# Scan tiles one column wider: a shifted C product, state copies on ScalarE, and a fourth B product on GpSimd

## The chip, the cores and the metric

The kernel runs on one core of a Trainium2 chip. A core has five engines that work side by side, each through its own queue in order: TensorE (PE) multiplies matrices, VectorE (DVE), ScalarE (ACT) and GpSimd (POOL) do elementwise work, and SyncE (SP) issues most of the DMAs. [...] The metric is the device time of one execution in microseconds; the median of three runs before the change is 10453.09 us (10444.79 to 10455.69).

## What is computed

The reference chains four image layers over a tensor of 4 x 192 x 64 x 64 fp32. Layer 0 runs two Mamba state space models over 4 sequences of 4096 tokens (the second over flipped channels) and adds them. Layer 1 is a normed Mamba, a depthwise convolution and an MLP. Layers 2 and 3 are a gated convolution and a windowed product with an MLP; the change does not touch them. The core of each Mamba is a recurrence over tokens for 384 channels and 16 states:

```python
dt = softplus(dt @ dt_w.T + dt_b)
def step(h, inp):
    dt_t, B_t, C_t, x_t = inp
    dA = exp(dt_t[..., None] * A)
    h = dA * h + (dt_t * x_t)[..., None] * B_t[:, None, :]
    y = einsum('bdn,bn->bd', h, C_t)
    return h, y
```

## The kernel before

Three stages follow each other: `two_mambas` (layer 0), `mamba_block` (layer 1), `conv_and_windows` (layers 2 and 3). The first two share the classes `Mamba` and `Scans`.

**Tiling.** A sequence is cut into pieces of T = 512 tokens. One Mamba over one piece is a unit; layer 0 has 32 pieces and two Mambas, so 32 pairs of units that alternate m0, m1, m0, m1; layer 1 has 32 units. The 384 x 16 states of a unit lie in NQ = 12 "quads" k of 128 partitions (16 channels x 8 states) by 4 columns j. Between pieces of a sequence the last state of each quad is kept in `state[:, k, :]`, 128 x 4.

**One quad.** `load` (L605) brings the rows of dt and of dt * x, spread over partitions, by DMA from DRAM (`dtE`, `dtxE`, two buffers each). `product` (L639) multiplies dtxE, 128 x 4 x 512, by B into a tile: on VectorE, with B in PSUM, into `h` (three buffers), or, for quads k in `shared`, on GpSimd, with a copy of B in SBUF (`Bs`, loaded at L628), into `h_apart` (two buffers in layer 0, one in layer 1). `decay` (L646) makes dA for one column on ScalarE, in one of three PSUM buffers; `step` (L652) scans that column on VectorE, in place, starting from `state`. After the four columns `read` copies the last states to `state` (L664) and multiplies the tile by C in place (L665), both on GpSimd. `sum` (L674) adds over states on TensorE, some steps later, and `skip` (L696, L698) and `gate` (L704) finish every fourth quad.

In layer 0, m0 has `shared` (3, 7, 11) and m1 (2, 5, 8, 11); in layer 1 it is (3, 7, 11).

**The order.** It is written out by hand. `Scans.run` counts steps i, four to a quad. A step issues the decay for i + 2, then the scan of i. At column 2 it issues the GpSimd product of the quad that begins at i + 6, if that one is shared. At column 3 it issues `read`, and the VectorE product of the next quad unless that is shared. Then it issues what was put down for this step with `at` (sums, skips, gates), and then `Behind.tick` adds work of other parts (norm, projection, convolution, output), from lanes, within a budget of TensorE and ScalarE time. A `burst` (a Silu or Softplus of 128 x 1536 between two loads of ScalarE's function table) is only issued at an `edge`: the step i for which i + 2 is the last column of a quad and the next quad is not shared. So `shared` moves bursts too.

Of the work beside the scans, three lines matter here: L861, ScalarE's passes of the layer-0 norm; L865, a 128 x 4 GpSimd instruction between two of these passes; and L517, a GpSimd product of 128 x 1536 (dt * x) that follows the Softplus burst (L516) of a unit to come. L471 is a GpSimd copy of three columns into the front of `raw`, whose other columns ScalarE writes (L483).

Of the kernel before, what the change touches and what calls it, by code (L numbers as in the profile page):

```python
# [14 lines left out]
F32 = mybir.dt.float32  # L15
AF = mybir.ActivationFunctionType
ALU = mybir.AluOpType
# [5 lines left out]
C = 192  # L23
# [10 lines left out]
T = 512  # L34
# [89 lines left out]
def near_convolution():  # L124


    sign = sedenion_signs()
    a, b = ([1 if v == "+" else -1 for v in text] for text in (X_SIGNS, W_SIGNS))
    s, rest = [], []
    for k in range(16):  # L130
        row = [sign[i][k] * a[i] * b[i ^ k] for i in range(16)]
        s.append(1 if sum(row) >= 0 else -1)
        rest.append([i for i in range(16) if row[i] != s[k]])
    return a, b, s, rest
# [285 lines left out]
class Mamba:  # L420
# [211 lines left out]
    def product(self, u, k):  # L632
        apart = k in self.shared
        if apart:
            h = self.work.tile([128, 4, T], F32, name="h_apart", bufs=1 if self.summed else 2)
        else:
            h = self.work.tile([128, 4, T], F32, name="h", bufs=3)
        engine, B = (self.nc.gpsimd, "Bs") if apart else (self.nc.vector, "B")
        engine.tensor_tensor(  # L639
            h, u["rows", k // 2, 1], u[B, k % 2].unsqueeze(1).broadcast_to([128, 4, T]), ALU.mult  # L640
        )
        u["h", k] = h

# [6 lines left out]
    def step(self, u, k, j):  # L650
        h = u["h", k]
        self.nc.vector.tensor_tensor_scan(  # L652
            h[:, j, :],
            u.pop(("dA", k, j)),
            h[:, j, :],
            self.state[:, k, j : j + 1],
            ALU.mult,
            ALU.add,
        )

    def read(self, u, k):

        nc, h = self.nc, u["h", k]
        nc.gpsimd.tensor_copy(self.state[:, k, :], h[:, :, T - 1])  # L664
        nc.gpsimd.tensor_tensor(  # L665
            h, h, u["C", k % 2].unsqueeze(1).broadcast_to([128, 4, T]), ALU.mult
        )

    def sum(self, u, k):
        i, h = k % 4, u.pop(("h", k))  # L670
        if i == 0:
            u["ys"] = self.psum_y.tile([128, T], F32, name="y")
        for j in range(4):
            self.nc.tensor.matmul(  # L674
                u["ys"][32 * j : 32 * j + 32, :],
                self.ex.gather[:, i // 2, :],
                h[:, j, :],
                start=(i == 0),
                stop=(i == 3 and self.summed),
                skip_group_check=not self.summed,  # L680
            )
        if i == 3 and not self.summed:
            c = k // 4
            self.nc.tensor.matmul(
                u["ys"],
                self.skip_w[:, c, :],
                u["xc"][:, c, :],
                start=False,
                stop=True,
                skip_group_check=True,  # L690
            )
# [15 lines left out]
class Scans:  # L707
# [49 lines left out]
    def step(self, i, n):  # L757
        m, u, k, j = self.tile(i)
        _, _, first, before, after = self.units[i // (4 * NQ)]
        if k == j == 0:  # L760
            if first:
                self.nc.vector.memset(m.state, 0.0)
            before()
        to = i + (12 if k % 2 else 8)
        if j == 0 and to < n:
            m2, u2, k2, _ = self.tile(to)
            self.behind.force(lambda: "rows" in u2)
            m2.load(u2, k2 // 2, k % 2)
        if i + self.AHEAD < n:
            m2, u2, k2, j2 = self.tile(i + self.AHEAD)  # L770
            m2.decay(u2, k2, j2)
        m.step(u, k, j)
        if j == 1 and k >= NQ - 2 and i + 8 < n:
            m2, u2, _, _ = self.tile(i + 8)
            m2.spread(u2, k - (NQ - 2))
            self.behind.budget -= 0.85
        if j == 2 and i + 6 < n:
            m2, u2, k2, _ = self.tile(i + 6)
            if k2 in m2.shared:
                self.behind.force(lambda: ("Bs", k2 % 2) in u2)  # L780
                m2.product(u2, k2)
        if j == 3:
            self.behind.force(lambda: ("C", k % 2) in u)
            m.read(u, k)
            if k >= NQ - 2 and i + 8 < n:
                m2, u2, _, _ = self.tile(i + 8)
                o = k - (NQ - 2)
                self.behind.add(0, m2.spread_C(u2, o), Piece())
            if i + 1 < n:
                m2, u2, k2, _ = self.tile(i + 1)  # L790
                if k2 not in m2.shared:
                    m2.product(u2, k2)
            added, skipped, gated = (4, 6, 8) if m.summed else (7, 10, 10)
            if k % 4 == 0 and not m.summed or k + 2 in m.shared and m.summed:
                added += 1 if m.summed else 2
            self.at(i + added, lambda: self.sum(m, u, k))
            if k % 4 == 3:
                c = k // 4
                self.at(i + skipped, lambda: self.skip(m, u, c))
                self.at(i + gated, lambda: m.gate(u, c))  # L800
                if c == ND - 1:
                    self.at(i + gated, lambda: self.gated(u, after))
# [14 lines left out]
def two_mambas(tc, x, gb_ap, m_ins, ex_aps, out, at_first):  # L817

    nc = tc.nc
    nq = T // 128  # L820
    with ExitStack() as ctx:
# [15 lines left out]
        mambas = [  # L837
            Mamba(
                nc, f"m{i}", 4, m_ins[i], const, work, const, work, psum_y, psum_a, dram, ident, ex, behind,
                ((3, 7, 11), (2, 5, 8, 11))[i], xcs=4,  # L840
            )
            for i in range(2)
        ]
# [381 lines left out]
def conv_and_windows(tc, x, sums, packs, aps, walsh, out):  # L1225
# [13 lines left out]
    with ExitStack() as ctx:  # L1239
# [147 lines left out]

        xn, kept, stored, outs = {}, {}, {}, {}
        read, projected, through, closed = set(), set(), set(), set()
        made, back = set(), set()  # L1390
        settled = [0] * NB
# [273 lines left out]
        for b in range(NB):  # L1665
            lanes.until(lambda: settled[b] == NP)
            if b == 0:
                w2 = work.tile([128, NH * T], F32, name="w2", tag="hid", bufs=1)
                weights(w2[: C // 4, : 4 * 3 * 128], NB - 1, NB)
                for j in range(16):  # L1670
                    if w_sign[j] > 0:
                        nc.scalar.activation(sed[:, :, j, :], sed[:, :, j, :], AF.Copy, scale=-1.0)
            if b:
                fetch(b)
            if b + 1 < NB:
                lanes.add(2, prepare(b + 1))
            lanes.add(4, inverse(b))
            for g in range(NP):
                spectrum(b, g)
            for k in range(NP):  # L1680
                n = b * NP + k
                reached[b] = k
                lanes.until(lambda: n < 2 or n - 2 in projected)
                lanes.until(lambda: n < X3 or n - X3 in closed)
                x3 = work.tile([128, 3, NWIN], F32, name="x3", bufs=X3)
                nc.sync.dma_start(x3, kept.pop((b, k)))
                lanes.add(0, project(b, k, product(b, k), x3))
# [4 lines left out]
def program(ctx, tc, aps, packs, out):  # L1692
# [6 lines left out]
    def m_ins(name):  # L1699
        return packs[name], aps[name], aps[f"{name}_in_w"], aps[f"{name}_dt_w"]  # L1700

    walsh = dram.tile([128, 16 + NP, C], F32, name="walsh")
    two_mambas(
        tc,
        aps["x"],
# [141 lines left out]
```

## Time and profile before

| | |
|---|---|
| median of 3 runs | 10453.09 us |
| the profiled execution | 10447.22 us, span 10445.3 us |
| granted TensorE clock, mean | 0.864 |
| scans, 3328 on h and 1280 on h_apart | 1266 and 1262 ns each |
| C products, 832 on h and 320 on h_apart | 4532 and 4530 ns each |
| state copies, 832 and 320 | 192 and 190 ns each |
| B products, VectorE 832, GpSimd 320 | 2261 and 4616 ns each |
| decays dA, 4608 | 686 ns each |

A line of a timeline gives the start and length in microseconds, the engine, the line of the kernel, the operation, the tile written and the tiles read; in brackets how long the engine sat idle before it and whom it waited for. Lengths of neighbours overlap a little, so distances from start to start are what adds up. A line of waits gives who waited for whom, the microseconds in total, the times and the longest. A line of windows gives a stretch, its length, then the busy time (and number of instructions) of PE, its weight loads, DVE, ACT and POOL, the clock, the DMA share and GB/s.

### The profile page before, as it was taken

What the parts mean: (1) busy time and instruction counts of PE and PEld (TensorE: products, weight loads), DVE (VectorE), ACT (ScalarE), POOL (GpSimd) and SP (SyncE); (2) the same over time, 40 slices, a digit from 0 to 9 for tenths busy, and PEclk for the clock granted to TensorE, in tenths of its full rate; (3) what the DMA queues carried; (4) which work ended last, traced back from release to release, by engine and by line L of the source; (5) the groups of instructions that cost most, each with busy time, mean ns of one, the idle gap of its engine ahead of it and who ended that gap; (6) DMA issues with size and microseconds to landing.
All of it is one profiled execution on the core that took longest, in us unless ns stands there. A gap on an engine that the chain in (4) does not pass through costs nothing. (4 is left out here: it accounts for less than half of the span.)

```text
span 10445.3 us, 96318 instructions
## 1 busy us (share of the span) xinstructions
PE 8260.7 (79%) x30264; PEld 3448.8 (33%) x30264; DVE 8758.5 (84%) x7569; ACT 6522.9 (62%) x9370; POOL 7937.2 (76%) x3712
## 2 busy tenths in 40 slices
PE   6777777777777777777558888888888886989898
PEld 2222222222222222222123333333333333545455
DVE  8999999999999999999968888888888876555552
ACT  5766666666666666666556767677776653444433
POOL 6999999999999999999969888888888861101100
PEclk8888888888888888888668999999999987999999
DMA  7777777777777777777656556556555543122110
GB/s 187 198 189 197 192 194 194 197 197 192 190 197 194 193 195 194 199 190 193 165 141 159 158 153 162 153 153 161 153 158 152 154 110 74 44 61 53 41 41 19
DMA packets 1020423, 1605.58 MB, mean 154 GB/s; under 512 B 250965, under 2 KB 284073, under 8 KB 1019401
## 3 DMA queue, kind: packets, MB, share of 16 engines
q1 hardware_dynamic: 1018912, 1596.13, 58.5%
q8 instruction: 240, 3.93, 0.2%
q10 hardware_dynamic: 1000, 3.30, 0.1%
q14 instruction: 271, 2.21, 0.1%
HBM read 1379.66 MB, written 219.41 MB: 153 GB/s over the span
## 5 line engine op out<-in xcount | busy, mean ns | idle before, releaser
L652 DVE TENSOR_TENSOR_SCAN h<-dA,m_state,h 128x512 f32<-128x512 f32 x3328 | 4041.3, 1266 | 231.9 <-ACT dA L646 157.7
L646 ACT ACTIVATE dA<-dtE,m_A 128x512 f32<-128x512 f32 x4608 | 3110.3, 686 | 1633.7 <-DVE h L652 1301.1
L665 POOL TENSOR_TENSOR h<-h,C 128x2048 f32<-128x2048 f32 x832 | 3770.4, 4532 | 72.2 <-DMA C<-r_bc 5.2
L639 DVE TENSOR_TENSOR h<-dtxE,B 128x2048 f32<-128x2048 f32 x832 | 1881.3, 2261 | 67.6 <-DMA dtxE<-r_dtx 66.6
L652 DVE TENSOR_TENSOR_SCAN h_apart<-dA,m_state,h_apart 128x512 f32<-128x512 f32 x1280 | 1554.0, 1262 | 135.4 <-ACT dA L646 123.2
L639 POOL TENSOR_TENSOR h_apart<-dtxE,Bs 128x2048 f32<-128x2048 f32 x320 | 1477.2, 4616 | 0.2 <-PE y L674 0.2
L665 POOL TENSOR_TENSOR h_apart<-h_apart,C 128x2048 f32<-128x2048 f32 x320 | 1449.6, 4530 | 25.8
L674 PE MATMUL y<-h,gather 128*32 128x512 f32 x6656 | 1006.3, 680 | 545.5 <-POOL h L665 399.1
L1382 POOL TENSOR_TENSOR d<-d,rs 128x512 f32<-128x512 f32 x64 | 86.3, 1349 | 1596.7 <-DVE rs L1381 1575.7
L476 PE MATMUL ps_in<-xT,m_in_w 96*128 96x512 f32 x1536 | 925.6, 757 | 322.5 <-ACT z L483 307.3
L560 PE MATMUL ps_conv<-raw,m_conv 128*128 128x512 f32 x1536 | 697.1, 599 | 6.7 <-POOL raw L471 4.2
L476 PEld LDWEIGHTS ps_in<-xT,m_in_w 96*128 96x128 f32 x1536 | 360.3, 244 | 895.3 <-issue 413.2
L476 PE MATMUL ps_in<-xn,m_in_w 96*128 96x512 f32 x768 | 426.7, 695 | 163.1 <-ACT z L483 75.3
L1131 PE MATMUL ps_dw<-strip,dw 96*96 96x512 f32 x1152 | 526.3, 602 | 9.3 <-ACT xc L588 8.5
L674 PEld LDWEIGHTS y<-h,gather 128*32 128x32 f32 x6656 | 140.3, 113 | 1179.4 <-issue 536.7
L377 PE MATMUL ps_h<-xn,t 96*128 96x512 f32 x768 | 422.7, 695 | 131.8 <-ACT xc L588 67.8
L1547 PE MATMUL sed_ps<-xn,sed 64*128 64x256 f32 (+3 forms) x2944 | 488.0, 404 | 7.0 <-DVE y L1566 7.0
L494 PE MATMUL ps_x<-xc,m_pack 128*68 128x512 f32 x576 | 373.8, 802 | 130.5 <-ACT xc L490 130.5
L517 POOL TENSOR_TENSOR raw<-dt,xc 128x1536 f32<-128x1536 f32 x96 | 324.7, 3383 | 185.9 <-ACT dt L516 183.6
L646 ACT ACT_TABLE_LOAD x345 | 442.6, 1283 | 14.8 <-DMA dtE<-r_dt 8.5
L507 PE MATMUL ps_dt<-dbl,m_dt_w 68*128 68x512 f32 x576 | 319.0, 658 | 155.8 <-ACT dt L510 109.2
L664 POOL COPY m_state<-h 128x4 f32<-128x4 f32 x832 | 159.5, 192 | 369.8 <-DVE h L652 362.4
(196 smaller groups left out, 11899.8 us busy)
## 6 DMA issues: line engine op xcount, KB each, us to landing
dtE<-r_dt SPq DMA_DIRECT2D x2304, 256.0 KB, 5.2
dtxE<-r_dtx SPq DMA_DIRECT2D x2304, 256.0 KB, 4.3
r_dt<-dt SPq DMA_DIRECT2D x96, 768.0 KB, 3.9
r_dtx<-raw SPq DMA_DIRECT2D x96, 768.0 KB, 6.2
C<-r_bc SPq DMA_DIRECT2D x192, 256.0 KB, 6.2
Bs<-r_bc SPq DMA_DIRECT2D x128, 256.0 KB, 7.1
x<-x SPq DMA_DIRECT2D x64, 384.0 KB, 3.6
img<-x SPq DMA_DIRECT2D x28, 512.0 KB, 8.4
```

The source lines that it names most:

```text
L377: nc.tensor.matmul(ps, self.w1[:, k, bass.ts(m, 128)], x[:, k, :], start=(k == 0), stop=(k == 1))
L476: nc.tensor.matmul(ps, self.in_w[:, k, bass.ts(e, 128)], xn[:, k, :], start=(k == 0), stop=(k == 1))
L494: nc.tensor.matmul(ps, self.x_w[:, d, :], xc[:, d, :], start=(d == 0), stop=(d == ND - 1))
L517: nc.gpsimd.tensor_tensor(dtx, dt, xc, ALU.mult)
L560: nc.tensor.matmul(ps, self.conv[:, d, j, :], raw[:, d, j : j + T], start=(j == 0), stop=(j == K - 1))
L639: engine.tensor_tensor(h, u["rows", k // 2, 1], u[B, k % 2].unsqueeze(1).broadcast_to([128, 4, T]), ALU.mult)
L646: self.nc.scalar.activation(dA, u["rows", k // 2, 0][:, j, :], AF.Exp, scale=self.A[:, k, j : j + 1])
L652: self.nc.vector.tensor_tensor_scan(h[:, j, :], u.pop(("dA", k, j)), h[:, j, :], self.state[:, k, j : j + 1], ALU.mult, ALU.add,)
L665: nc.gpsimd.tensor_tensor(h, h, u["C", k % 2].unsqueeze(1).broadcast_to([128, 4, T]), ALU.mult)
L674: self.nc.tensor.matmul(u["ys"][32 * j : 32 * j + 32, :], self.ex.gather[:, i // 2, :], h[:, j, :], start=(i == 0), stop=(i == 3 and self. ...
L1131: nc.tensor.matmul(ps, dw[:, k, j, :], s[:, k, dy : dy + rows, dx : dx + HW], start=(j == 0), stop=(j == 8),)
L1547: nc.tensor.matmul(out, sed[p, int(h is not None), i ^ position(k, s), cols], xn[b, g][p, c, :], start=group(t) not in begun, stop=left[gr ...
```

## The change

Both tiles, `h` and `h_apart`, get one column more: 513 in place of 512. The B product writes columns 1 to 512, and the scan works there. The C product reads columns 1 to 512 and writes columns 0 to 511, so column 512, the last state, survives it. The copy to `state` is no longer the first of two GpSimd instructions in `read`; it is an own method, `keep`, on ScalarE, put down for two steps later. The sum reads columns 0 to 511. In layer 0, m0 gets the `shared` of m1. Layer 1 keeps its own.

```diff
-            h = self.work.tile([128, 4, T], F32, name="h_apart", bufs=1 if self.summed else 2)
+            h = self.work.tile([128, 4, T + 1], F32, name="h_apart", bufs=1 if self.summed else 2)
         else:
-            h = self.work.tile([128, 4, T], F32, name="h", bufs=3)
+            h = self.work.tile([128, 4, T + 1], F32, name="h", bufs=3)
         engine, B = (self.nc.gpsimd, "Bs") if apart else (self.nc.vector, "B")
         engine.tensor_tensor(
-            h, u["rows", k // 2, 1], u[B, k % 2].unsqueeze(1).broadcast_to([128, 4, T]), ALU.mult
+            h[:, :, 1:], u["rows", k // 2, 1], u[B, k % 2].unsqueeze(1).broadcast_to([128, 4, T]), ALU.mult
         )
...
         self.nc.vector.tensor_tensor_scan(
-            h[:, j, :],
+            h[:, j, 1:],
             u.pop(("dA", k, j)),
-            h[:, j, :],
+            h[:, j, 1:],
...
+    def keep(self, u, k):
+        self.nc.scalar.copy(self.state[:, k, :], u["h", k][:, :, T])
+
     def read(self, u, k):
 
         nc, h = self.nc, u["h", k]
-        nc.gpsimd.tensor_copy(self.state[:, k, :], h[:, :, T - 1])
         nc.gpsimd.tensor_tensor(
-            h, h, u["C", k % 2].unsqueeze(1).broadcast_to([128, 4, T]), ALU.mult
+            h[:, :, :T], h[:, :, 1:], u["C", k % 2].unsqueeze(1).broadcast_to([128, 4, T]), ALU.mult
         )
...
-                h[:, j, :],
+                h[:, j, :T],
...
             m.read(u, k)
+            self.at(i + 2, lambda: m.keep(u, k))
...
-                ((3, 7, 11), (2, 5, 8, 11))[i], xcs=4,
+                (2, 5, 8, 11), xcs=4,
```

## The prediction

> **What bounds the kernel now.** I read the page first (busy shares and slices), then the windows of two stages, then the waits inside the first stage, and last the timeline of one pair of units, because only there can one see which wait ends last.
>
> ```profile
> PE 8260.7 (79%) x30264; PEld 3448.8 (33%) x30264; DVE 8758.5 (84%) x7569; ACT 6522.9 (62%) x9370; POOL 7937.2 (76%) x3712
> DVE  8999999999999999999968888888888876555552
> POOL 6999999999999999999969888888888861101100
> ...
> 2000.00:3000.00 1000.00, 746.78 (x2541) 284.22 (x2543) 967.26 (x743) 680.87 (x1044) 955.29 (x406) 0.82 0.74 195
> 6000.00:7000.00 1000.00, 876.77 (x2810) 324.80 (x2809) 852.71 (x690) 703.74 (x932) 870.23 (x438) 0.93 0.59 157
> ```
>
> The changed code runs in two stages. In the two-mamba stage (about 75 to 5207 us) VectorE is busy 97% and GpSimd 96%; in the mamba-block stage (to about 8540 us) TensorE, VectorE and GpSimd all stand near 87% and none is full. After that GpSimd is nearly idle and nothing changed runs. So the first stage is a VectorE stage with GpSimd right behind it, and there the waits count:
>
> ```profile
> DVE h_apart L652 <- ACT dA L646: 73.7, 32, 2.5
> DVE h_apart L652 <- POOL h_apart L639: 10.2, 29, 0.5
> ...
> POOL raw L517 <- ACT dt L516: 72.7, 42, 2.3
> POOL m_state L664 <- DVE h L652: 71.8, 82, 2.0
> ...
> ACT xs L861 <- POOL shift L865: 116.7, 29, 4.1
> ```
>
> These are from 200 to 5000 us. VectorE's main loss is about thirty waits of some 2.4 us, one a pair. The timeline shows their source (unit m0 begins with the B product at 2161.78):
>
> ```profile
> 2161.78 2.26 DVE L639 TENSOR_TENSOR h<-dtxE,B 128x2048 f32<-128x2048 f32 x1
> 2168.87 2.26 DVE L639 TENSOR_TENSOR h<-dtxE,B 128x2048 f32<-128x2048 f32 x1
> ...
> 2184.18 3.63 DVE L652 TENSOR_TENSOR_SCAN h_apart<-dA,m_state,h_apart 128x512 f32<-128x512 f32 x3 [0.35 <-POOL h_apart L639]
> 2184.36 4.52 POOL L665 TENSOR_TENSOR h<-h,C 128x2048 f32<-128x2048 f32 x1
> ...
> 2188.85 0.22 POOL L865 TENSOR_SCALAR shift<-shift 128x4 f32<-128x4 f32 x1
> 2189.02 0.18 POOL L664 COPY m_state<-h 128x4 f32<-128x4 f32 x1
> 2189.11 0.45 ACT L861 ACTIVATE xs<-xt,shift 128x192 f32<-128x192 f32 x1 [4.03 <-POOL shift L865]
> 2189.29 4.57 POOL L665 TENSOR_TENSOR h<-h,C 128x2048 f32<-128x2048 f32 x1
> ...
> 2190.26 1.28 DVE L652 TENSOR_TENSOR_SCAN h_apart<-dA,m_state,h_apart 128x512 f32<-128x512 f32 x1 [2.45 <-ACT dA L646]
> ```
>
> A tiny norm instruction (L865) stands behind a 4.5 us C product in GpSimd's queue; ScalarE stops for it 4.03 us, the next decay dA is late, VectorE stands still 2.45 us.
>
> **A budget of one pair.** From start to start in this timeline, four scans take 4.72 us (2164.15 to 2168.87), a VectorE B product 2.37 (2161.78 to 2164.15), a gating product 0.59. Unit m1 (8 of its 12 B products on VectorE) then needs 12 x 4.72 + 8 x 2.37 + 3 x 0.59 = 77.37 us. It took 77.32 (2084.46 to 2161.78): pure VectorE. Unit m0 (9 on VectorE) needs 79.74 and took 83.06 (to 2244.84): 3.3 us are stalls, of which the timeline shows 0.20 + 0.35 + 2.45. A pair is 160.4 us. GpSimd occupies 155.5 of it (160.4 less its waits, (72.7 + 71.8) / 29.9 pairs = 4.8).
>
> [...]
>
> **The change part by part.**
> 1. State copies leave GpSimd. Each is 0.19 us busy and, from its start to that of the C product behind it, 0.27 us (2189.02 to 2189.29). 24 a pair free 6.5 us of GpSimd; 12 a unit free 3.2 us in the mamba block.
> 2. The copies go to ScalarE. No row shows a 128x4 SBUF copy there. Nearest: a 128x4 ACTIVATE with a pointer bias (ln_rs, 243 ns), an accumulator read (187 ns, but 0.09 us from start to start). [...] Bounds 0.1 to 0.25; I take 0.1, so 2.4 us a pair on an engine 68% busy. The copy comes in step i + 2, behind the decay for i + 4, which must itself wait for scan i + 1; the scan it needs is therefore over, and it waits for nothing. Behind it stand decays and, in the same step, the bursts (table load, 1.48 us, table load). After a burst VectorE has 0.2 to 0.4 us of cover (0.97 us from dA's start at 2199.95 to its scan at 2200.92, of which 0.69 is dA), so 0.1 is mostly hidden. Uncovered it would be 0.1 x 6 bursts = 0.6 us a pair.
> 3. Must the copy wait for the C product, which writes the same tile before it? It reads column 512, the product writes 0 to 511. Such a case is in the trace: ScalarE writes columns 3 and up of raw while GpSimd's halo copy of columns 0 to 2, earlier in the program, is still to come:
>
> ```profile
> 1165.86 0.58 ACT L483 COPY raw<-ps_in 128x512 f32<-128x512 f32 x1
> ...
> 1169.17 0.20 POOL L471 COPY raw<-m_halo 128x9 f32<-128x9 f32 x1
> ```
>
> So columns are told apart, and no wait arises. If it did, ScalarE would stop for up to 4.5 us in each of 24 quads.
> 4. m0 gives a fourth B product to GpSimd: VectorE -2.37 us a pair, GpSimd +4.6 (its products at 2044.40, with the next start at 2049.00). GpSimd then needs 155.5 - 6.5 + 4.6 = 153.6 us a pair, VectorE 2 x 77.37 = 154.7. It fits, barely.
> 5. What moves with it. m0 gets m1's order: B2, C0, C1, then L517, L865, C2, B5. From the m1 tail at 2168.8: B2 to 2173.4, C0 2177.9, C1 2182.4, L517 2185.8, L865 2186.0 against 2189.1 now. ScalarE reached its wait at 2185.1, so it loses 0.9 instead of 4.03 us, and VectorE, which wants that dA at 2187.8 at the earliest, next to nothing. GpSimd no longer waits for dt (burst one edge later, as in m1). B5 and B8 end 0.2 to 0.4 us before their scans by the same count, B2 and B11 1 to 3 us. So of 3.3 us of stall I keep 1.1 (the 0.20, the burst delay, near misses of B5 and B8).
> 6. One more Bs load a unit of m0: 32 x 256 KB on SP, 0.60 us of issue each, about 0.26 MB more beside the 31 MB a pair (160.4 us at 195 GB/s). m1 already does this; it lands in 7.1 us, long before B2. Nothing.
> 7. The wider tiles. TensorE reads raw at odd columns (ps_conv, 592 ns median) as fast as aligned h (y, 617). VectorE writes strip in rows starting at odd columns in 689 ns against 668 for an aligned product: 0. GpSimd's C product is the unknown: now it reads and writes rows 513 apart. Of four rows with 1536 elements, the one with aligned inputs and odd output rows takes 3438 ns (L517, two-mamba stage), the others 3082 (L597, input rows 513 apart), 3252 and 3267. So odd rows look neutral to 10% faster; the other reading, that odd output rows cost the 171 ns between the two L517, would be +0.23 for 2048 elements, and more with odd reads as well. I take 0; bounds -0.45 and +0.35 us each.
> 8. The mamba block: GpSimd frees 3.2 us of about 100 a unit, but waits for VectorE already (m_state, 225 us), so the copy is no bound there; TensorE's 45 us of waits for C products may shrink by 32 x 0.27 = 9 us, and 32 x 12 copies on ScalarE (VectorE waits for dA 165 us there) give about as much back. 0, within 20.
>
> Sum: 32 pairs x (2.37 + 2.2) = 146 us. The profiled execution took 10447.2 us (span 10445.3); 10447 - 146 = 10301. The median of the three runs, 10453.1, lies 6 us above it, hence 10307.
>
> **The rivals.**
> Stall stays: L865 is no earlier, because the norm's place or GpSimd's lag moves, and only VectorE's product is saved: 32 x 2.37 = 76 us, 10377. For it: GpSimd's slack falls to 1 us a pair; against: m1 runs in this order without a stall.
> GpSimd gets fuller than it is (slower): the C product at odd columns costs more. From +0.05 us each GpSimd (153.6 + 24 d) takes over from VectorE, at +0.28 the gain is gone, at +0.35 a pair is 162.0: 32 x 1.6 = 51, and some 15 in the mamba block: 10519. For it: the two L517; against: L597 and L595.
> C product faster: GpSimd clears all stalls, 32 x 5.7 = 182, and TensorE waits less in the block, 10: 10261.
> The copies make ScalarE late after most bursts, and GpSimd's fuller m0 adds near misses of B: about 10440.
>
> **How the numbers follow.** Forecast 0.48 (own range 10270 to 10350), stall stays 0.25 (0.04 of it within no change), GpSimd fuller 0.15, C faster 0.08, ScalarE late 0.04. A change of under 0.2% (21 us) can't be told from none. Faster 0.48 + 0.21 + 0.08 = 0.77, same 0.08, slower 0.15. The range from 10250 to 10455 leaves out the slower case and a few hundredths at either end.
>
> **What would show it.** In the changed profile: m0 and m1 both near 77 to 78.5 us; ACT xs <- POOL shift far under 117 us; VectorE's 2.45 us waits gone; L664 gone from GpSimd and a ScalarE copy of 0.16 to 0.25 us in its place with no wait for POOL; C product within 0.1 us of 4.53; GpSimd over 97% busy. I am wrong if the C product's mean moves by more than 0.1 us, if the copy waits, or if VectorE waits for h_apart B products beyond 1 us a pair.

## The result and the profile after

The changed kernel takes 10357.01 us (median of 4 runs, 10353.09 to 10358.94) beside 10453.28 us for the kernel before: ratio 0.9909, interval 0.9892 to 0.9926. The forecast was 10307. So 96 us came where 146 were expected. The profiled span shrank by 88.6 us, from 10445.3 to 10356.7 (the execution profiled before was 6 us under its median, the one after 1.5 us above), and the first normed image of the mamba block (the first L310) and its last strip part this by stage: the two-mamba stage is 109.4 us shorter, the mamba block 23.8 us longer, the last stage 3.0 us shorter.

First the page's busy times of the changed kernel, then its windows in the two stages:

```profile
PE 8231.6 (79%) x30264; PEld 3420.2 (33%) x30264; DVE 8680.6 (84%) x7537; ACT 6649.9 (64%) x10522; POOL 7450.7 (72%) x2592
```

```profile
2000.00:3000.00 1000.00, 759.22 (x2615) 286.33 (x2615) 976.90 (x756) 713.82 (x1211) 922.98 (x272) 0.85 0.75 199
6000.00:7000.00 1000.00, 863.81 (x2763) 318.15 (x2762) 836.12 (x675) 704.61 (x1035) 792.77 (x312) 0.94 0.56 154
```

GpSimd lost 486 us of work, ScalarE gained 127. In the two-mamba stage VectorE is busy 98% and GpSimd 92%; the prediction had GpSimd above 97%. In the block VectorE and TensorE are both busy for a smaller share than before: they wait more there. The reason for the 92% stands in the groups of instructions (line, operation, tiles and count; then busy time in all and the mean in ns; then idle time before them and its cause):

```profile
L667 POOL TENSOR_TENSOR h<-h,C 128x2048 f32<-128x2048 f32 x800 | 3336.1, 4173 | 721.5 <-DVE h L652 546.6 <-issue 82.7 <-DMA dtxE<-r_dtx 43.7
L639 POOL TENSOR_TENSOR h_apart<-dtxE,Bs 128x2048 f32<-128x2048 f32 x352 | 1596.0, 4534 | 27.0 <-DMA Bs<-r_bc 24.0 <-ACT dA L646 2.8
...
L662 ACT COPY m_state<-h 128x4 f32<-128x4 f32 x800 | 145.6, 182 | 0.0
...
L662 ACT COPY m_state<-h_apart 128x4 f32<-128x4 f32 x352 | 63.5, 180 | 2.8 <-DVE h_apart L652 2.8
```

The C product went from 4532 to 4173 ns, which nothing had asked for, and GpSimd now waits for VectorE. The copy on ScalarE lasts 0.18 us and never waits for GpSimd; it waits for VectorE 2.8 us in all. The waits from 200 to 5000 us:

```profile
POOL h L667 <- DVE h L652: 219.8, 146, 2.3
DVE h L652 <- ACT dA L646: 39.5, 34, 1.3
DVE h_apart L652 <- ACT dA L646: 17.1, 24, 0.8
DVE h_apart L652 <- POOL h_apart L639: 2.3, 3, 1.0
ACT xs L864 <- POOL shift L868: 15.4, 29, 0.5
```

ScalarE's wait for the norm's little GpSimd instruction fell from 116.7 to 15.4 us, and VectorE's thirty waits of 2.45 us are gone. Some 60 us of shorter ones are left. In the timeline of one unit m0, from its first product at 2124.93 to that of m1 at 2204.38, they look like this:

```profile
2124.93 2.27 DVE L639 TENSOR_TENSOR h<-dtxE,B 128x2048 f32<-128x2048 f32 x1
...
2160.89 0.32 ACT L921 COPY o<-ps_out 128x192 f32<-128x192 f32 x1 [2.65 <-PE ps_out L913]
2161.83 2.46 DVE L652 TENSOR_TENSOR_SCAN h_apart<-dA,m_state,h_apart 128x512 f32<-128x512 f32 x2 [0.80 <-ACT dA L646]
2162.34 0.18 ACT L662 COPY m_state<-h 128x4 f32<-128x4 f32 x1
2162.53 1.28 ACT L534 ACT_TABLE_LOAD   x1
...
2165.22 0.53 ACT L864 ACTIVATE xs<-xt,shift,rs 128x192 f32<-128x192 f32 x1
2167.79 2.46 DVE L652 TENSOR_TENSOR_SCAN h<-dA,m_state,h 128x512 f32<-128x512 f32 x2 [1.32 <-ACT dA L646]
...
2204.38 2.27 DVE L639 TENSOR_TENSOR h<-dtxE,B 128x2048 f32<-128x2048 f32 x1
```

This m0 took 79.45 us (83.06 before), and the m1 ahead of it, from 2047.61 to 2124.93, 77.32 us as before. The two stalls, 0.80 and 1.32 us, are all that tells m0 from m1 now. Both are ScalarE being late: before the first it had waited 2.65 us for TensorE's ps_out; the second comes after a burst, with a norm pass right behind it.

### The profile page after: what moved, and what is told of

It is laid out like the page before. It is cut to its first block, busy times and chain, and to the rows that moved or that the text cites. A ratio compares the mean times of both kernels' runs of the same rounds, so it can differ in the third digit from the quotient of the medians.

```text
span 10356.7 us, 96620 instructions
## 1 busy us (share of the span) xinstructions
PE 8231.6 (79%) x30264; PEld 3420.2 (33%) x30264; DVE 8680.6 (84%) x7537; ACT 6649.9 (64%) x10522; POOL 7450.7 (72%) x2592
## 5 line engine op out<-in xcount | busy, mean ns | idle before, releaser
L652 DVE TENSOR_TENSOR_SCAN h<-dA,m_state,h 128x512 f32<-128x512 f32 x3200 | 3884.6, 1267 | 256.9 <-ACT dA L646 186.3
L667 POOL TENSOR_TENSOR h<-h,C 128x2048 f32<-128x2048 f32 x800 | 3336.1, 4173 | 721.5 <-DVE h L652 546.6
L639 DVE TENSOR_TENSOR h<-dtxE,B 128x2048 f32<-128x2048 f32 x800 | 1809.8, 2262 | 66.0 <-DMA dtxE<-r_dtx 66.0
L652 DVE TENSOR_TENSOR_SCAN h_apart<-dA,m_state,h_apart 128x512 f32<-128x512 f32 x1408 | 1709.5, 1263 | 85.5 <-ACT dA L646 80.2
L639 POOL TENSOR_TENSOR h_apart<-dtxE,Bs 128x2048 f32<-128x2048 f32 x352 | 1596.0, 4534 | 27.0 <-DMA Bs<-r_bc 24.0
L667 POOL TENSOR_TENSOR h_apart<-h_apart,C 128x2048 f32<-128x2048 f32 x352 | 1468.9, 4173 | 108.0 <-DVE h_apart L652 106.8
L476 PE MATMUL ps_in<-xT,m_in_w 96*128 96x512 f32 x1536 | 846.5, 691 | 97.1 <-ACT z L483 57.2
L476 PE MATMUL ps_in<-xn,m_in_w 96*128 96x512 f32 x768 | 440.9, 715 | 171.9 <-ACT z L483 77.2
L476 PEld LDWEIGHTS ps_in<-xT,m_in_w 96*128 96x128 f32 x1536 | 320.9, 224 | 697.7 <-issue 365.2
L904 PE MATMUL ps_out<-m_pack,xc 128*128 128x192 f32 x1536 | 334.9, 370 | 264.3 <-DVE xc L698 187.1
L377 PE MATMUL ps_h<-xn,t 96*128 96x512 f32 x768 | 419.4, 691 | 137.5 <-ACT xc L588 70.1
L676 PE MATMUL y<-h_apart,gather 128*32 128x512 f32 x2816 | 429.9, 686 | 60.2 <-DVE xc L698 44.9
L517 POOL TENSOR_TENSOR raw<-dt,xc 128x1536 f32<-128x1536 f32 x96 | 325.3, 3389 | 190.7 <-ACT dt L516 189.9
```

The source lines that it names most:

```text
L377: nc.tensor.matmul(ps, self.w1[:, k, bass.ts(m, 128)], x[:, k, :], start=(k == 0), stop=(k == 1))
L476: nc.tensor.matmul(ps, self.in_w[:, k, bass.ts(e, 128)], xn[:, k, :], start=(k == 0), stop=(k == 1))
L639: engine.tensor_tensor(h[:, :, 1:], u["rows", k // 2, 1], u[B, k % 2].unsqueeze(1).broadcast_to([128, 4, T]), ALU.mult)
L652: self.nc.vector.tensor_tensor_scan(h[:, j, 1:], u.pop(("dA", k, j)), h[:, j, 1:], self.state[:, k, j : j + 1], ALU.mult, ALU.add,)
L667: nc.gpsimd.tensor_tensor(h[:, :, :T], h[:, :, 1:], u["C", k % 2].unsqueeze(1).broadcast_to([128, 4, T]), ALU.mult)
L676: self.nc.tensor.matmul(u["ys"][32 * j : 32 * j + 32, :], self.ex.gather[:, i // 2, :], h[:, j, :T], start=(i == 0), stop=(i == 3 and self ...
```

## The experiments

Two questions: which part made the gain, and where the missing 50 us are. One view is that the parts add up, each with a gain of its own. The rival: they only work together. The table puts all runs side by side. "Need" is the prediction's own count of VectorE's work a pair (77.37 us for a unit with 8 B products on VectorE, 79.74 with 9, 75.0 with 7), "waits" are VectorE's waits from 200 to 5000 us divided by the pairs in that stretch, and "pair" is the measured mean distance of the silu bursts of 26 pairs. "Stage" is the start of the first L310, "block" the distance from there to the last strip, each from one profiled execution. The ratio is to the kernel before as it was measured beside each run.

| run | need | waits | pair | stage | block | time | ratio to before, interval |
|---|---|---|---|---|---|---|---|
| before | 157.1 | 3.23 | 160.35 | 5244.1 | 3310.7 | 10453.28 | 1 |
| after | 154.7 | 1.97 | 156.57 | 5134.7 | 3334.5 | 10357.01 | 0.9909, 0.9892 to 0.9926 |
| e1 no fourth product | 157.1 | 3.24 | 160.40 | 5245.4 | 3332.3 | 10469.43 | 1.0021, 1.0013 to 1.0029 |
| e2 only fourth product | 154.7 | 5.87 | 160.44 | 5254.3 | 3304.1 | 10453.27 | 1.0002, 0.9994 to 1.0011 |
| e3 copies on GpSimd | 154.7 | 1.53 | 156.06 | 5118.1 | 3327.4 | 10339.24 | 0.9895, 0.9880 to 0.9909 |
| e7 slow C product | 154.7 | 2.11 | 156.48 | 5136.2 | 3345.6 | 10368.94 | 0.9921, 0.9906 to 0.9936 |
| e10 fast products | 154.7 | 1.62 | 156.09 | 5122.8 | 3334.8 | 10341.85 | 0.9894, 0.9878 to 0.9911 |
| e13 five of twelve | 150.0 | 6.67 | 157.00 | 5142.6 | 3313.0 | 10350.12 | 0.9909, 0.9894 to 0.9924 |
| e14 block undone | 154.7 | 2.00 | 156.47 | 5130.1 | 3324.8 | 10340.98 | 0.9900, 0.9885 to 0.9915 |
| e17 tiles in block | | | | 5125.5 | 3325.0 | 10340.48 | 0.9900, 0.9884 to 0.9917 |
| e12 best of each | 154.7 | 1.54 | 156.08 | 5120.8 | 3304.2 | 10315.29 | 0.9874, 0.9858 to 0.9891 |
| e8 copy in block | | | | 5241.7 | 3317.9 | 10445.10 | 0.9993, 0.9985 to 1.0002 |
| e8x two copies | | | | 5242.9 | 3401.6 | 10529.12 | 1.0074, 1.0059 to 1.0089 |

Need and waits add up to the measured pair within 0.4 us in all ten kernels for which the table has them. So a change in this stage is read by two questions: what does VectorE have to do, and how long does it stand still?

**e1: the changed kernel without the fourth product in m0.**

```diff
-                (2, 5, 8, 11), xcs=4,
+                ((3, 7, 11), (2, 5, 8, 11))[i], xcs=4,
```

> The change without its fourth B product: m0 keeps 3, 7, 11 on GpSimd; shift and ScalarE copies stay. Theory A (order and room together make the gain): in m0 the small norm instruction still stands behind L517, B3 and C1, and L517 waits for dt, so it comes only about 0.9 us earlier (one C product and one copy shorter); VectorE's 2.45 us wait falls to about 1.5; the pair goes from 160.4 to about 159.3, the two-mamba stage gains 35 us, the mamba block loses the 24 us that the change lost there: about 10440. Theory B (the faster C product alone clears the stall): the pair falls to 157.4, 96 us less 24: about 10380.

The time, 10469.43, lies above what either theory gave: nothing is gained, though GpSimd is relieved to 87% from 1000 to 3000 us. Its waits:

```profile
DVE h_apart L652 <- ACT dA L646: 54.5, 31, 1.8
DVE h L652 <- ACT dA L646: 31.4, 60, 1.0
...
ACT xs L864 <- POOL shift L868: 95.4, 29, 3.3
```

GpSimd's free time did not bring the norm's instruction L868 forward. The timeline shows why:

```profile
2175.10 3.43 POOL L517 TENSOR_TENSOR raw<-dt,xc 128x1536 f32<-128x1536 f32 x1 [2.97 <-ACT dt L516]
2178.49 4.51 POOL L639 TENSOR_TENSOR h_apart<-dtxE,Bs 128x2048 f32<-128x2048 f32 x1
2182.95 4.16 POOL L667 TENSOR_TENSOR h<-h,C 128x2048 f32<-128x2048 f32 x1
2187.09 0.23 POOL L868 TENSOR_SCALAR shift<-shift 128x4 f32<-128x4 f32 x1
```

GpSimd stands idle 2.97 us until the Softplus burst has made dt, and then L868 still has a dt * x product, a B product and a C product ahead of it. In the changed kernel it comes straight behind L517. ScalarE's wait went only from 116.7 to 95.4 us, and VectorE got a second kind of wait, 31.4 us where the kernel before has 8.7. The sum of its waits stayed: 96.8 us in both. The freed time alone does not end the stall.

**e2: the kernel before with the fourth product alone**, the same line edited the other way.

> The kernel before with only m0's set changed to 2, 5, 8, 11: no shift, copies on GpSimd. Theory A: GpSimd needs 155.5 + 4.6 = 160.1 us a pair, more than VectorE's 154.7, so GpSimd becomes the bound, VectorE waits for h_apart products, the pair is 160 to 161: 10440 to 10475. Theory B (the new order alone cures the late norm instruction, GpSimd has enough room): pair about 157, about 10345 to 10370, as the mamba block is untouched.

```profile
ACT xc L565 <- PE ps_conv L560: 302.1, 175, 3.6
...
DVE h L652 <- ACT dA L646: 128.6, 103, 1.9
...
DVE h_apart L652 <- ACT dA L646: 42.3, 49, 1.6
```

VectorE has its 2.37 us a pair less to do, and waits 2.64 us more. Theory A's figure holds, though VectorE waits for decays and not, as it said, for h_apart products (2.4 us in all). GpSimd is busy 98% from 1000 to 3000 us: ScalarE waits long for TensorE's convolution, and VectorE for its decay. The new order alone does not cure the norm's late instruction either: it stands straight behind L517 here too, but GpSimd comes to both late, and ScalarE still waits for it 86.3 us. That GpSimd's late C products hold TensorE's queue is the likely link; I did not test it by itself. Neither part alone is worth anything here, and both together are worth 96 us. The rival holds.

**e3: the changed kernel with the copies back on GpSimd**, but behind the C product, which the wider tile allows.

```diff
     def read(self, u, k):
...
+        nc.gpsimd.tensor_copy(self.state[:, k, :], h[:, :, T])
...
-            self.at(i + 2, lambda: m.keep(u, k))
```

> The change with the state copies on GpSimd, behind the C product, none on ScalarE. Theory C (the copies on ScalarE cost the 24 us in the mamba block): the block goes back from 3334 to about 3311 us, the two-mamba stage stays at 157.1 us a pair or gains 0.2 from ScalarE: about 10330. Theory D (the block is slower because C products end earlier and shift what ScalarE and TensorE meet): the block stays near 3334, all about 10357. If the copies also made VectorE's 0.80 and 1.33 us waits in the two-mamba stage, these go and the pair falls to 155.2: 10270.

VectorE's waits fall from 1.97 to 1.53 us a pair, which makes 14 us, and the stage ends 16.6 us earlier in this profile. Over all the profiles of this stage's two forms it ended at 5118 to 5123 us with the copies on GpSimd (e3, e10, e12) and at 5125 to 5136 with them on ScalarE (after, e7, e14, e17). The pair is 156.06 to 156.09 us with the former and 156.47 to 156.57 with the latter. So that place costs about 11 to 16 us, and GpSimd has room for them. The room is about what the quicker product gives, 24 x 0.36 = 8.6 us a pair against 6.5 for the copies; no run tried the copies there with a slow product. The block took 3327.4 us, between theory C's value and theory D's.

**e5: a probe of the GpSimd product**, four times each ahead of everything, with one read start changed at a time. Nothing it computes is used.

```diff
+            nc.gpsimd.tensor_tensor(even, even, by(c0), ALU.mult)
+            nc.gpsimd.tensor_tensor(odd[:, :, :T], odd[:, :, 1:], by(c0), ALU.mult)
...
+            nc.gpsimd.tensor_tensor(far[:, :, :T], far[:, :, 8:], by(c0), ALU.mult)
...
+            nc.gpsimd.tensor_tensor(even, even, by(c1), ALU.mult)
```

> The changed kernel with a bare row of GpSimd products of 128 x 2048 ahead of everything, four of each layout, outputs unused. Theory E (rows of 512 read at a start that differs from the second operand's by an odd column save time): 513 apart, read 1 to 512 and write 0 to 511: 4.17 us; 513 apart in place: 4.2 to 4.4; 520 apart (aligned, shifted by 8): 4.53; plain tile with C at an odd start: 4.2. Theory F (it is the pattern of four separate rows in place of one run of 2048): every padded tile, aligned ones too, takes 4.17, the plain tile 4.53 whatever C's start. Theory G (it is the distance of the write from the read): only the shifted ones, 1, 2 and 8 columns, are faster, those in place are not. The 128 x 4 copies on ScalarE: 0.18 us in both layouts.

The view of single lines (count, then shortest, median and longest in ns); rows are 512 columns apart in p_even, 513 in p_odd, 520 in p_far, and L1733 is the plain tile with C read from column 1:

```profile
L1724 POOL TENSOR_TENSOR p_even<-p_even,p_c x4: 4492/4493/4493, 16.5 to 212.5; 128x2048 f32<-128x2048 f32 x4
...
L1725 POOL TENSOR_TENSOR p_odd<-p_odd,p_c x4: 4147/4150/4150, 21.0 to 216.9; 128x2048 f32<-128x2048 f32 x4
...
L1730 POOL TENSOR_TENSOR p_far<-p_far,p_c x4: 4492/4492/4492, 41.9 to 237.8; 128x2048 f32<-128x2048 f32 x4
...
L1733 POOL TENSOR_TENSOR p_even<-p_even,p_c x4: 3810/3810/3810, 55.3 to 251.3; 128x2048 f32<-128x2048 f32 x4
```

Theories F and G fail: a shift by 8 columns does nothing (L1730: 4492), nor does where the result goes (an odd output start took 4493). E had the right kind of cause, but not the distances that save. What counts is how the two reads start relative to each other: C moved by one column makes the product 0.683 us shorter over four rows, 0.171 a row. Rows 513 apart save 0.343, two rows' worth. All the forms tried fit one rule, that a row is short, by 0.171 us, where the first read starts 2 or 3 columns after the second, counted modulo 4; why, no run shows. The same rule fits the four durations of 1536 elements in part 7 of the prediction: 3438 ns with no short row of three, 3267 and 3252 with one, 3082 with two. L517 is quicker in the block (3267 ns against 3438) because dt lies there in rows 513 apart, not slower elsewhere because of where it writes.

**e7: the changed kernel with the C product slow again**, by tiles 8 columns wider and not 1.

```diff
-            h = self.work.tile([128, 4, T + 1], F32, name="h", bufs=3)
+            h = self.work.tile([128, 4, T + 8], F32, name="h", bufs=3)
...
-            h[:, :, :T], h[:, :, 1:], u["C", k % 2].unsqueeze(1).broadcast_to([128, 4, T]), ALU.mult
+            h[:, :, :T], h[:, :, 8:], u["C", k % 2].unsqueeze(1).broadcast_to([128, 4, T]), ALU.mult
```

> The changed kernel with its tiles 8 columns wider instead of one, written 8 to the left, so that the C product should take the 4.49 us that the probe measured for this form; all else is as in the changed kernel. Theory 'the C product's speed was part of it': GpSimd's work of a pair of units goes from 144.5 to 144.5 + 24 x 0.32 = 152 us, close to VectorE's 154.7, and waits come back: 10385 to 10440. Rival 'its speed is slack': GpSimd stood idle for 8 per cent and only ScalarE is waited for, so 10357 within 10.

Its C products take 4540 ns, as before the change. Its window:

```profile
1000.00:3000.00 2000.00, 1523.96 (x5192) 567.21 (x5190) 1955.63 (x1512) 1429.95 (x2429) 1957.29 (x542) 0.84 0.76 200
```

GpSimd is busy 98% (1957 of 2000 us; 1846 in the changed kernel), VectorE 98% in both, and the stage ends 1.5 us later. In this stage the quicker product was slack. The run is 12 us longer, 2 more than the rival allowed, and 11 of them lie in the block; its ratio's interval overlaps with that of the changed kernel.

**e10: the other way, every GpSimd product quick.** The copies as in e3, tiles 8 columns wider and used from column 1, C and Bs read from column 2.

```diff
-            v = self.work.tile([128, T], F32, name=f"{n}{o}", bufs=bufs)
+            v = self.work.tile([128, T + 2], F32, name=f"{n}{o}", bufs=bufs)[:, 2:]
```

> The copies on GpSimd behind the C product as in the run e3, and all of GpSimd's products (C and B) laid out so that both reads differ by 2 or 3 columns modulo 4 in every row: C 4.17 to 3.81, B 4.53 to 3.81 us. GpSimd's work of a pair falls by 24 x 0.36 + 8 x 0.72 = 14 us. Theory 'VectorE and ScalarE bound the pair now': no gain beyond 10 us on 10339. Rival 'GpSimd's speed still sets it': the pair goes from 156.3 towards VectorE's 154.7, 10339 - 32 x 1.6 = 10290.

C products took 3818 ns and GpSimd's B products 3821, as the rule says, and GpSimd's busy share fell to 85% (1707 of 2000 us). The pair stayed at 156.09 (e3: 156.06). GpSimd's speed does not bound this stage any more.

**e13: five of twelve B products on GpSimd in both mambas**, with these quick products, a third buffer for `h_apart` in that stage, and the block as before.

```diff
-                (2, 5, 8, 11), xcs=4,
+                (2, 4, 6, 8, 10), xcs=4,
```

> Meant to be faster than both: the two-mamba stage with GpSimd's products in the fast layout of e10, copies on GpSimd, and 5 of 12 B products on GpSimd in both mambas; the block as before. Theory 'VectorE bounds the pair': its need falls by 2 x 2.26 us from 154.7 to 150.2, GpSimd's rises to 24 x 3.82 + 10 x 3.82 + 8 + 24 x 0.19 = 142 us, so the pair goes from 156.3 to 151.5 to 153: two-mamba stage 105 to 155 shorter, time 10180 to 10230 with the block at 3311. Rival 'ScalarE's or TensorE's chain bounds it now': the pair stays above 155 and the time above 10290.

```profile
ACT xc L566 <- PE ps_conv L561: 450.9, 183, 4.3
...
DVE xc L703 <- PE y L691: 76.9, 53, 1.7
...
DVE h_apart L653 <- ACT dA L647: 60.2, 42, 2.2
...
DVE h_apart L653 <- POOL h_apart L640: 44.1, 51, 2.1
DVE h L653 <- ACT dA L647: 21.7, 54, 1.4
```

VectorE has 4.7 us a pair less to do, and waits 5 us more: for y, for decays, for GpSimd's products. The rival's figure holds. With VectorE's need at 154.7 us the best pair, 156.06, is within 1.4 us of it; less need has so far come back as waits.

**e8 and e8x: the mamba block's 24 us.** The kernel before, with one or two ScalarE copies of 128 x 4 added for every quad of the block (the texts below say step) at the place of the new one; nothing reads them.

```diff
+    def idle_copy(self, k):
+        if self.summed:
+            self.nc.scalar.copy(self.spare, self.A[:, k, :])
...
+            self.at(i + 2, lambda: m.idle_copy(k))
```

> The kernel before with one ScalarE copy of 128 x 4 added for every step of the mamba block (A to a spare tile, nothing reads it), at the place where the changed kernel has its copy; its own copies stay on GpSimd. Theory 'the copy on ScalarE is what the block gave back': the block goes from 3311 to 3330 to 3336 us and the time to 10473 (10465 to 10480). Rival 'the block's loss comes from the tiles or from GpSimd's order': within 5 of the kernel before, 10453.

> As the run before it, with two such copies for each step in place of one. Theory 'the block's unit locks to a whole number of the 3.41 us stretches in which TensorE's clock is held': the first copy already put every unit on 102.4 us, so the second costs little: the block within 6 us of that with one copy. Rival 'each copy costs what it delays': twice the rise, about 10495 if one copy gives 10473.

With one copy the time is not above that of the kernel before, so the copy alone did not cost the block its 24 us here; its 7 us on the block lie within the spread told below. With two, both theories failed: the block is 91 us longer, neither the same nor twice as much. TensorE's two waits in the MLP of a unit, 1.75 and 2.83 us in the kernel before, are now 2.09 and 3.14:

```profile
7233.68 2.70 PE L377 MATMUL ps_h<-xn,t 96*128 96x512 f32 x4 [2.09 <-ACT hid L382]
7289.78 6.90 PE L377 MATMUL ps_h<-xn,t 96*128 96x512 f32 x8 [3.14 <-ACT xc L589]
```

Here such waits cost more than their own length, as the durations behind them show. The same eight products of ps_h, in two units of the kernel before (first fence) and one of the changed one (second):

```profile
7241.43 3.70 PE L377 MATMUL ps_h<-xn,t 96*128 96x512 f32 x8 [2.83 <-ACT xc L588]
...
7341.82 5.40 PE L377 MATMUL ps_h<-xn,t 96*128 96x512 f32 x8 [2.83 <-ACT xc L588]
```

```profile
7249.25 5.40 PE L377 MATMUL ps_h<-xn,t 96*128 96x512 f32 x8 [2.92 <-ACT xc L588]
```

After the same idle time TensorE needs 3.70 or 5.40 us. The trace records the granted clock, and windows over the two units of the kernel before, with one inside the second, show it (the figure after the five engines):

```profile
7241.43:7245.13 3.70, 3.70 (x9) 1.76 (x10) 1.95 (x2) 1.88 (x3) 3.22 (x3) 1.00 0.74 178
7341.82:7347.22 5.40, 5.40 (x9) 2.35 (x10) 1.94 (x2) 1.88 (x3) 4.85 (x5) 0.68 0.42 109
7342.40:7345.81 3.41, 3.41 (x6) 1.35 (x5) 1.36 (x2) 1.30 (x3) 3.30 (x2) 0.50 0.46 122
```

In the longer case the clock is halved for 3.41 us, from 0.58 us after the restart. The traces record two values of the granted clock, 1.00 and 0.50, and in the kernel before all its changes lie on one grid of 3.413 us through the whole run; so do those of the changed one. The time of the eight products goes with the place on this grid where the restart falls: of the 24 units of the kernel before, all with an idle time of 2.82 or 2.83 us, 6 restart 1.10 to 1.53 us behind a point of the grid and take 3.70 us, the other 18 restart elsewhere on it and take 5.40 us (13 units) or 6.77 to 7.09 (5). What makes the clock fall, no run tested. The restarts of neighbouring units of this kernel are 99.3 to 105.8 us apart, and many fall well and badly by turns. In the changed one the restart comes 0.09 us later and was slow (5.40 us) in all 24 units, and of the 20 distances 13 are 102.4 or 102.5 us. That is 30.0 steps of the grid, so such a unit meets it in the same place again and again: in seven neighbours from 6217.8 us on the half clock begins 0.94, 0.54, 0.41, 0.34, 0.31, 0.30 and 0.58 us after the restart. What holds a unit there, no run tested; e8, with the same idle time of 2.92 us, keeps that distance in 8 of 20 cases only and has three quick restarts, so the premise of the theory before e8x, all units on 102.4 us, did not hold.

The products of the norm and the projection around ps_h meet the half clock too: in the kernel before, four of the norm's (L308) took 1.88 us from 5463.51 on, at a clock of 1.00, and 2.96 us from 5671.12 on, at 0.64. Together with ps_h they were busy 1002.5 us before and 1018.7 after (L476 ps_in 426.7 and 440.9, L377 ps_h 422.7 and 419.4, L308 mean 153.1 and 158.4). But this sum does not explain the block by itself: e8 has the lowest, 985.3, and a block of 3317.9 us. The windows of the whole block, before, after, e12 and e14, show more:

```profile
5244.10:8554.80 3310.70, 2814.08 (x8965) 1047.63 (x8966) 2767.55 (x2227) 2265.74 (x3002) 2817.34 (x1405) 0.90 0.58 153
5134.70:8469.20 3334.50, 2805.93 (x8965) 1035.63 (x8966) 2767.38 (x2227) 2307.73 (x3386) 2616.47 (x1021) 0.91 0.56 152
5120.80:8425.00 3304.20, 2806.94 (x8965) 1042.70 (x8966) 2767.54 (x2228) 2266.14 (x3002) 2817.66 (x1405) 0.91 0.59 153
5130.10:8454.90 3324.80, 2833.46 (x8965) 1057.03 (x8966) 2767.24 (x2228) 2266.17 (x3002) 2818.74 (x1405) 0.90 0.58 152
```

e12 and e14 (below) have the same code in the block, that of the kernel before. e14's is 21 us longer and TensorE's busy time in it 27 us, its idle time 6 us less: there the pace makes the difference. In the changed kernel TensorE is busy 8 us less than before and idle 32 us more. So its 24 us show as waits, and how many of these a slow restart set off is open.

**e14 and e17: the changed kernel with the block's code undone**, wholly (plain tiles, product in place, copy on GpSimd ahead of it), or only the copy brought back to GpSimd.

```diff
+        if self.summed:
+            nc.gpsimd.tensor_copy(self.state[:, k, :], h[:, :, T])
...
-            self.at(i + 2, lambda: m.keep(u, k))
+            if not m.summed:
+                self.at(i + 2, lambda: m.keep(u, k))
```

> The changed kernel with the mamba block alone as it was: there plain tiles, the C product in place, the copy on GpSimd ahead of it. Theory 'the 24 us that the block gave back are due to the change's own code in the block': block 3304 to 3318 us and 10357 - 24 = 10333 (10325 to 10342). Rival 'the block is only hit at another moment of TensorE's clock because the stage ahead of it ends earlier': block stays near 3334 and the time within 5 of 10357.

> The changed kernel with, in the mamba block, the copy back on GpSimd ahead of the C product, and the wider tiles kept: no ScalarE copy there. With e8 (ScalarE copies alone: block 3318) it parts the block's 24 us. Theory 'the ScalarE copy and the rest add up': block 3334 - 7 = 3327, time 10350. Rival 'the copy on ScalarE matters only together with the tiles': block near 3311, time 10333.

Both blocks took 3325 us, between the two theories' values for e14. With the old block code, five profiles (before, e2, e12, e13, e14) gave 3304 to 3325 us; with the new one, three (after, e1, and e5, whose probe runs ahead of everything) gave 3332 to 3334.5. So the code seems to matter, but the same code varies by 21 us from one kernel to another, with different work ahead of it. Against this spread the 24 us cannot be shared out between the copy and the tiles.

**e12: each stage in its shortest form**, the two-mamba stage as in e3 and the block's code as before.

> Each stage in the form that was shortest so far: in the two-mamba stage the wider tiles and the copies on GpSimd behind the C product (as in e3, stage ended at 5118), in the mamba block the code of the kernel before (as in e14). If the stages' times add up: 5118 + a block of 3304 to 3325 + 1887 = 10309 to 10330 of span, time 10312 to 10335, ratio 0.987 to 0.989. If the block's time is mostly a matter of the moment at which it meets TensorE's clock: anywhere from 10312 to 10345, no shorter than e3's 10339 for certain.

10315.29 us, ratio 0.9874 (0.9858 to 0.9891): the fastest kernel of all here, 135 us under the kernel before in the same comparison (10450.34). Against the changed kernel the two ratios differ by 0.35 points, and their intervals just part. The stages' times added up, as the first forecast had it, though the time lies within the rival's range too. e3, e10, e14 and e17 lie near 10340, but their intervals overlap with that of the changed kernel, so none of them is shown to be faster than it.

## Why the prediction was right and where it failed

The side, faster, was right, and the path was right: VectorE bounds the two-mamba stage, the norm's instruction held ScalarE, and m1's order in m0, with the room on GpSimd that it needs, ended that. By the prediction's parts:

- **Parts 1 and 4, GpSimd's room.** Right in effect. With the C product at its old speed, as the sum assumed, GpSimd is 98% busy and the stage is 1.5 us longer (e7). The "over 97%" was not seen in the changed kernel only because the product got quicker.
- **Parts 2 and 3, the copy.** No wait for the C product arose, 0.18 us each as bounded. The 0.1 us taken as the price of one was the author's estimate; in the changed kernel's timeline it is 0.09 us from its start to that of a norm pass (2136.34 to 2136.43), 0.19 to that of a table load (2162.34 to 2162.53). "Mostly hidden" was too kind: 0.44 us a pair, from e3, of the 0.6 that was given as the uncovered price.
- **Part 5, the stalls.** The mechanism was right, the size was not: "of 3.3 us of stall I keep 1.1" measured 1.97 (2.12 in the m0 shown, which so missed the "77 to 78.5 us"; m1 kept to it). The near misses of B5 and B8 that it listed are almost nothing (2.3 us in 4800), but ScalarE's two delays of 0.80 and 1.32 us remained: the first was not on the list, and of the second only "the burst delay" without a size. A pair fell by 3.78 us, not by 4.57: 25 us less over 32 pairs. A further 12 us is the difference between 32 x 3.78 and the stage's 109.4. It lies at the start, before the pairs are regular: from the first Silu of `xc` (L490) to the ninth, four pairs, only 3.8 us were gained in place of 15.
- **Part 7, the wider tiles.** "I take 0" was wrong as to the duration, 0.36 us less each, though within the bounds; for the stage it was 0 all the same. The two L517 were read as a sign of what odd output rows cost, but e5 shows that the reads make that difference. The prediction's own test, "wrong if the C product's mean moves by more than 0.1 us", went off, and the rival built on it, that a quicker product clears all stalls, fell: e10 made it quicker still and gained nothing.
- **Part 8, the block.** "0, within 20" was +24. That GpSimd's freed time would gain nothing there was right. That the copy on ScalarE and TensorE's shorter waits for C products cancel was not: TensorE is idle 32 us more. The prediction also left out that TensorE's pace can differ with the same code: e14's block is 21 us longer than that of e12, with 27 us more of busy time on TensorE. How the 24 us divide is open.

The sum: 146 - 25 - 12 - 24 + 3 = 88, the span's 88.6.

The prediction put parts 1 and 4 into one budget for GpSimd, and that was needed: e1 and e2 are both worth nothing. Its rival "stall stays" gave 2.37 us a pair for the product without the cure. e2, on the old copies, comes nearest to that case, and there 2.64 us of new waits took it back.

## What to carry to other kernels

Write the budget of the bounding engine as need plus waits and ask of each edit which of the two it changes: here relief of the engine next to the bound was worth nothing until the bound's own need fell (e1: ratio 1.0021), and less need was worth nothing while the neighbour was full (e2: 1.0002). A short instruction behind a long one was brought forward by another order once its engine had the time for it (ScalarE's wait for it fell from 116.7 to 15.4 us): free time in the old order and the new order on a full engine both failed. In the block TensorE idled 2.83 us in each of 24 units, and the same eight products behind that took 3.70 us in 6 of them and 5.40 us or more in 18: price such a stage with a spread of its own.

## What the runs showed of the hardware

- The duration of GpSimd's product of 2048 columns depends on how its two reads start relative to each other: 4493, 4150 or 3810 ns, with equal work (e5).
- TensorE took 3.70 or 5.40 us for the same eight products after the same idle time of 2.83 us (two units of the kernel before). In the longer case its granted clock was 0.50 for 3.41 us, in the shorter one 1.00 throughout.
